# A graph-attention layer on one core: TensorE turns the edge features after k and q, three turns ahead

## The chip, the core and the metric

The kernel runs on one core of one Trainium2 chip. Its engines work side by side, each on its own list of instructions, in order: TensorE (PE: matrix products and transposes through the array, results in PSUM), VectorE (DVE), ScalarE (ACT), GpSimd (POOL) and SyncE (SP). They wait for one another through semaphores. SP issues nearly all plain transfers here, GpSimd the gathers. The metric is device time in microseconds: before the change 2678.94 us, the median of three runs (2676.61 to 2681.4).

## The reference

A graph has 12,500 nodes and 212,500 edges, sorted by destination. Nodes are normalized, and q and v are products of them; k is a product of the edges' features. Per edge and head (8 heads of 16) there are three logits: q of the source with k, q of the destination with k, and q of the source with q of the destination. Each goes through a softmax over the edges of one destination, and their sum weighs v.

```python
h = jnp.maximum(_layernorm(x, axis=-1), 0.0)
q = (node_h @ Wq.T + bq).reshape(N, NUM_HEADS, HEAD_DIM)
k = (edge_h @ Wk.T + bk).reshape(-1, NUM_HEADS, HEAD_DIM)
v = (node_h @ Wv.T + bv).reshape(N, NUM_HEADS, HEAD_DIM)
qs, qd = (q[src], q[dst])
in_m = jnp.sum(qs * k, axis=-1)
out_m = jnp.sum(qd * k, axis=-1)
diag_m = jnp.sum(qs * qd, axis=-1)
score = (_segment_softmax(in_m * SCALE, dst, N) + _segment_softmax(out_m * SCALE, dst, N) + _segment_softmax(diag_m * SCALE, dst, N)) * att
h = jax.ops.segment_sum(score[..., None] * v[dst], dst, num_segments=N)
out = h @ Wo.T + bo          # x + leaky_relu(out) is the result
```

## The kernel before

The kernel prepares q for all nodes and writes it to a table in HBM, then walks the edges in 415 turns of 512 edges (128 partitions by 4). Turn g belongs to stage t = g // 5 and stretch s = g % 5: the edges are cut into five long stretches, and a stage takes one block of each.

The instructions of an engine stand in the order in which the program makes them: `pin` chains each to the one before on its engine, so nothing is reordered by a scheduler. What a turn does for its 512 edges:

- `turn` (L1308, L1310): TensorE transposes four tiles of edge features `ea` into the one PSUM buffer `eT_ps`; ScalarE copies them to `eT` (three buffers).
- `project` (L1317, L1318): TensorE multiplies `eT` with wk, which gives k in one half of `qk_ps` (two buffers), and adds the bias.
- `spread_q` (L1326, L1329): TensorE multiplies one-hots `oh` of the destinations with a window of 42 nodes' q, which gives the destinations' q in the other half of `qk_ps`; ScalarE copies that half to `qd`.
- `logits` (L1337, L1339, L1340): VectorE multiplies the gathered source q `qq`, `qd` and k by pairs and sums over each head. This frees `qk_ps` for the turn after next.
- `one_hots` (L702, L703): two instructions on ScalarE, three turns ahead.

The order of the loop before is: transposes of turn g+2, k of g+1, the destinations' q of g+1, logits of g, one-hots of g+3. So TensorE's list has the transposes ahead of k, and ScalarE's list has the copy of features, then the copy to `qd`, then the one-hots.

Behind these five come odd jobs, which depend on s. They belong to earlier stages. At s = 0 TensorE transposes the first logits of a block (`turn_head`, L1368) and VectorE scans; at s = 1 VectorE scans backwards; at s = 2 TensorE transposes the maxima (`turn_max`, L1443), VectorE subtracts (L1452) and ScalarE takes exponentials (L1453); at s = 3 TensorE makes `d_ps` (L1485), from which ScalarE makes the selection `sel` (L1488, L1489); at s = 4 TensorE sums the edges of a node into `w_ps` (`to_rows`, L1499), ScalarE copies these to `rows` (L1504), which SP stores (L1520), and TensorE transposes logits (`turn_logits`, L1360). Work on nodes (`nodes_before`, `nodes_between`, for instance L1228, L1239, L1242, L1247) and on parts of the q table (L1619) is spread over the turns as well.

The gathers run 26 turns ahead: `gather(g + LOOK)` issues four indirect transfers from GpSimd (L711), each of 128 rows of q. They are tied to TensorE by hand. The dictionary `behind` keeps two of TensorE's instructions for each turn: entry 0 is its last product after `project`, entry 2 its last product after the odd jobs. In turn g the first of the four gathers waits for entry 0 of g, the third for entry 2 of g, and both entries of g were made in turn g-1:

```python
held = behind.get((g - LOOK, j), held)
...
behind[g + 1, 0] = pinned[products]
...
behind[g + 1, 2] = pinned[products]
```

SP's list holds, by turns, the load of edge features six turns ahead (`fetch_edges`, L691, six buffers `ea`), of windows (L685), and the stores of `rows`.

Of the kernel before, what the change touches and what calls it, by code (L numbers as in the profile page):

```python
# [472 lines left out]
def ordered_path(ctx: ExitStack, tc: tile.TileContext, flag, x, src, dst, edge_attr, edge_weight,  # L473
# [88 lines left out]
    def pin(inst):  # L562

        engine = str(inst.ins.engine)
        if engine in pinned:
            tc.add_manual_dep(inst.ins, pinned[engine], mybir.DependencyInfo(
                mybir.DependencyClass.NoSync, mybir.DependencyReason.DATA), reason="in order")
        pinned[engine] = inst.ins.name
        return inst
# [61 lines left out]
    end = S * G  # L631
# [5 lines left out]
    def load_sources(t):  # L637
        if t < G:
            sources[t] = load.tile([P, S, JN], I32, name="sources", bufs=IDX)
            pin(nc.sync.dma_start(  # L640
                sources[t], src[:end * BE].rearrange("(s b p j) -> p s b j", s=S, b=G, p=P)[:, :, t, :]))
# [80 lines left out]
    def raw_rectify(g):  # L722
        for j in range(JN):
            row = qqs[g][:, j, :]
            pin(nc.scalar.activation(row, row, AF.Relu, bias=raw["shift"][:, g, j:j + 1],
                                     scale=raw["inv"][:, g, j:j + 1]))
# [53 lines left out]
    with tc.tile_pool(name="prep", bufs=1) as prep, \  # L780
# [359 lines left out]
        for g in range(-2, GN):  # L1140
# [13 lines left out]
            for of in range(RAW):  # L1154
                turn = (5 * of - 30) // 4
# [35 lines left out]
    class Nodes:  # L1191
# [45 lines left out]
        def turn(self, to):  # L1237
            for b in range(self.n):
                pin(nc.tensor.transpose(to[:, b, :], self.h[:, b, :], ident))  # L1239
            if self.hT is None:  # L1240
                self.hT = fin.tile([P, JN, P], F32, name="hT")
            pin(nc.scalar.copy(self.hT[:, :self.n], to[:, :self.n]))  # L1242
# [57 lines left out]
    with tc.tile_pool(name="work", bufs=2) as work, \  # L1300
# [21 lines left out]
        def spread_q(g):  # L1322
            s, d = g % S, st[g // S]
            qd_ps = qks[g][:, 1]
            for j in range(JN):
                pin(nc.tensor.matmul(qd_ps[:, j, :], ohs[g][:, j * P:(j + 1) * P],  # L1326
                                     d["win"][:, s, :], start=(j == 0), stop=(j == JN - 1)))
            qds[g] = work.tile([P, JN, F], F32, name="qd")
            pin(nc.scalar.copy(qds[g], qd_ps))  # L1329
            del ohs[g]  # L1330

        def logits(g):
            s, t = g % S, g // S
            if s == 0:
                lTs[t] = scan.tile([P, JN, S, H3], F32, name="lT", bufs=4)
            prod = work.tile([P, JN, 3, F], F32, name="prod", bufs=1)
            pin(nc.vector.tensor_mul(prod[:, :, 0:2, :].rearrange("p j i f -> p i j f"),  # L1337
                                     qqs[g][:, None].to_broadcast([P, 2, JN, F]), qks[g]))
            pin(nc.vector.tensor_mul(prod[:, :, 2, :], qds[g], qks[g][:, 0]))  # L1339
            pin(nc.vector.tensor_reduce(lTs[t][:, :, s, :],  # L1340
                                        prod.rearrange("p j i (h d) -> p j (i h) d", d=DIM), AX.X,
                                        ALU.add))
            del qks[g], qds[g], qqs[g]
# [398 lines left out]
        project(0)  # L1742
        spread_q(0)
        turn(1)
        raw_rectify(SOON)
        for g in range(end):
            s, t = g % S, g // S
# [3 lines left out]
            fetch_edges(g + EDGES)  # L1751
            if s == 1:
                load_sources(t + IDX)
            if g + 2 < end:
                turn(g + 2)
            if g + 1 < end:
                project(g + 1)
                behind[g + 1, 0] = pinned[products]
                spread_q(g + 1)
            logits(g)  # L1760
            one_hots(g + 3)
            if s == 0:
# [157 lines left out]
```

## Time and profile before

| | |
|---|---|
| median of the runs | 2678.94 us |
| profiled execution | 2685.56 us, span 2683.8 us |
| PE, PEld | 1794.6 us (67%), 1479.8 us (55%) |
| DVE | 2046.8 us (76%) |
| ACT | 1397.2 us (52%) |
| POOL | 1587.5 us (59%) |
| granted TensorE clock, mean | 0.739 |
| HBM | 132 GB/s over the span |

PE stands for TensorE's products and transposes, PEld for its weight loads, which overlap them. "Idle before, releaser" in a row is the time in which the engine did nothing ahead of these instructions, and what ended most of it; "issue" means that the profile shows nothing to wait for, and "remote" that the releaser is not known. Ends of TensorE's products are modelled; those of the others are recorded. A view by windows gives the busy time of each engine in a stretch, with the number of its instructions.

### The profile page before, as it was taken

The numbers are of one execution on the slowest core, as the hardware profiler recorded it, in microseconds if no ns is written. First come the engines' busy times: TensorE is split into PE (matmuls) and PEld (weight loads), VectorE is DVE, ScalarE is ACT, GpSimd is POOL, SyncE is SP. The second block draws the span as 40 slices with busy tenths as digits, with TensorE's granted clock in tenths as the row PEclk, the third lists the DMA queues.
The fourth block names the chain that finished last, engine by engine and source line by source line (L and its number), as shares of the span: only waits on it lengthen the run. The fifth ranks groups of instructions, "written<-read, shape, count | busy, mean of one in ns | idle before, by whom it ended". The sixth has DMA issues, their size and how long they took to land.

```text
span 2683.8 us, 36827 instructions
## 1 busy us (share of the span) xinstructions
PE 1794.6 (67%) x10958; PEld 1479.8 (55%) x10958; DVE 2046.8 (76%) x2496; ACT 1397.2 (52%) x2663; POOL 1587.5 (59%) x1683
## 2 busy tenths in 40 slices
PE   3656766666566666676666766676767676766775
PEld 2455655555455545565555655565656565555664
DVE  4648887777787878787778877777877787778995
ACT  3647754454455554554545545455545554455672
POOL 6656566666666666666666666666666666666100
PEclk6767877777777777777777777766777677677786
DMA  6656444444555454454444444454444444444321
GB/s 184 175 159 169 124 129 136 136 128 133 141 146 135 127 151 135 135 139 136 127 130 129 133 130 129 131 136 130 115 135 134 125 129 131 133 129 129 112 87 53
DMA packets 379084, 355.75 MB, mean 133 GB/s; under 512 B 192913, under 2 KB 298779, under 8 KB 378669
## 3 DMA queue, kind: packets, MB, share of 16 engines
q1 hardware_dynamic: 309963, 238.05, 31.2%
q0 software_dynamic: 53184, 108.92, 15.5%
q10 hardware_dynamic: 15728, 6.33, 1.0%
q8 instruction: 90, 1.47, 0.2%
q14 instruction: 119, 0.97, 0.1%
HBM read 320.89 MB, written 32.17 MB: 132 GB/s over the span
## 4 chain that ended last, share of the span: by engine, by line
PE 39%; ACT 17%; DVE 16%; issue 12%; another core or an unknown queue 12%; DMA 1%; POOL 1%; DVEq 1%; SPq 0%; ACTq 0%; POOLq 0%
PE qk_ps L1317 11%; PE eT_ps L1308 8%; PE w_ps L1499 6%; DVE lT L1340 4%; DVE prod L1337 4%; PE qk_ps L1326 4%; ACT qd L1329 3%; ACT relb L702 3%; ACT oh L703 2%; ACT eT L1310 2%; DVE prod L1339 2%; PE node_ps L1247 2%; PE m_ps L1443 2%; PE l_ps L1360 1%
## 5 line engine op out<-in xcount | busy, mean ns | idle before, releaser
L711 POOL DMA_INDIRECT qq<-q_table,sources x1564 | 1482.0, 948 | 856.3 <-issue 375.1
L1337 DVE TENSOR_TENSOR prod<-qq,qk_ps 128x1024 f32<-128x1024 f32 x412 | 501.2, 1217 | 318.6 <-ACT qd L1329 185.1
L1340 DVE TENSOR_REDUCE lT<-prod 128x96 f32<-128x1536 f32 x415 | 727.5, 1753 | 14.3
L1317 PE MATMUL qk_ps<-wk,eT 128*128 128x128 f32 x3320 | 597.0, 337 | 72.2 <-issue 34.3
L1329 ACT COPY qd<-qk_ps 128x512 f32<-128x512 f32 x415 | 244.2, 589 | 731.2 <-remote 241.8
L1317 PEld LDWEIGHTS qk_ps<-wk,eT 128*128 128x128 f32 x3320 | 551.9, 250 | 90.8 <-issue 43.0
L1308 PE MATMUL eT_ps<-ident,ea 128*128 128x128 f32 x1660 | 347.1, 345 | 373.6 <-ACT eT L1310 169.0
L1308 PEld LDWEIGHTS eT_ps<-ident,ea 128*128 128x128 f32 x1660 | 241.9, 176 | 469.3 <-ACT eT L1310 193.5
L1310 ACT COPY eT<-eT_ps 128x512 f32<-128x512 f32 x415 | 240.0, 578 | 200.4 <-remote 114.3
L1499 PE MATMUL w_ps<-back,sel 128*126 128x144 f32 (+1 forms) x1296 | 229.3, 350 | 159.1 <-issue 141.7
L1499 PEld LDWEIGHTS w_ps<-back,sel 128*126 128x126 f32 (+1 forms) x1296 | 211.8, 240 | 173.5 <-issue 157.5
L702 ACT ACTIVATE relb<-relb,before 126x512 bf16<-126x512 bf16 x415 | 301.9, 728 | 0.0
L1339 DVE TENSOR_TENSOR prod<-qd,qk_ps 128x512 f32<-128x512 f32 x415 | 282.1, 680 | 0.0
L703 ACT ACTIVATE oh<-relb 126x512 bf16<-126x512 bf16 x415 | 261.3, 630 | 13.2
L1326 PE MATMUL qk_ps<-win,oh 126*128 126x128 bf16 x1660 | 194.8, 250 | 6.8 <-issue 6.8
L1326 PEld LDWEIGHTS <-oh 126*128 126x128 bf16 x1660 | 110.5, 109 | 32.4 <-issue 8.0
L1443 PE MATMUL m_ps<-ident,m 120*128 120x120 f32 x332 | 74.6, 360 | 68.9 <-issue 46.9
L1400 DVE TENSOR_TENSOR_SCAN l_ps<-far,carry,l_ps 120x512 f32<-120x512 bf16 x80 | 102.5, 1281 | 11.1 <-PE eT_ps L1308 7.5
L711 POOL DMA_INDIRECT qq<-in_x_dram,sources x84 | 80.0, 952 | 49.3 <-issue 22.3
L1452 DVE TENSOR_TENSOR back<-lT,m_ps 128x480 f32<-128x480 f32 x83 | 53.9, 650 | 70.9 <-remote 38.0
L1431 DVE TENSOR_TENSOR_SCAN m<-far,head,l_ps 120x512 f32<-120x512 bf16 x81 | 102.9, 1271 | 0.0
L1443 PEld LDWEIGHTS m_ps<-ident,m 120*128 120x128 f32 x332 | 52.3, 215 | 81.9 <-issue 57.7
(252 smaller groups left out, 1783.0 us busy)
## 6 DMA issues: line engine op xcount, KB each, us to landing
ea<-in_edge_attr_dram SPq DMA_DIRECT2D x415, 256.0 KB
relb<-rel_d SPq DMA_DIRECT2D x83, 630.0 KB
qq<-q_table,sources POOLq DMA_INDIRECT x1564
win<-q_table SPq DMA_DIRECT2D x415, 31.5 KB
far<-far_d SPq DMA_DIRECT2D x84, 120.2 KB
q_table<-q SPq DMA_DIRECT2D x24, 384.0 KB
sums<-rows SPq DMA_DIRECT2D x411, 7.9 KB
q_table<-xq SPq DMA_DIRECT2D x24, 256.0 KB
```

The lines of the kernel that those rows point to most:

```text
L702: pin(nc.scalar.activation(d, d, AF.Abs, bias=before[:K3]))
L703: pin(nc.scalar.activation(oh, d, AF.Relu, bias=1.0, scale=-1.0))
L711: rows = pin(nc.gpsimd.indirect_dma_start(out=qq[:, j, :], out_offset=None, in_=x if g < RAW else q_table, in_offset=bass.IndirectOffsetOn ...
L1308: pin(nc.tensor.transpose(eT_ps[:, j, :], eas[g][:, j * F:(j + 1) * F], ident))
L1310: pin(nc.scalar.copy(eT, eT_ps))
L1317: pin(nc.tensor.matmul(k_ps[:, j, :], eTs[g][:, j, :], wk, start=(j == 0), stop=False))
L1326: pin(nc.tensor.matmul(qd_ps[:, j, :], ohs[g][:, j * P:(j + 1) * P], d["win"][:, s, :], start=(j == 0), stop=(j == JN - 1)))
L1329: pin(nc.scalar.copy(qds[g], qd_ps))
L1337: pin(nc.vector.tensor_mul(prod[:, :, 0:2, :].rearrange("p j i f -> p i j f"), qqs[g][:, None].to_broadcast([P, 2, JN, F]), qks[g]))
L1339: pin(nc.vector.tensor_mul(prod[:, :, 2, :], qds[g], qks[g][:, 0]))
L1340: pin(nc.vector.tensor_reduce(lTs[t][:, :, s, :], prod.rearrange("p j i (h d) -> p j (i h) d", d=DIM), AX.X, ALU.add))
L1499: pin(nc.tensor.matmul(w_ps[:(hi - lo) * W, lo:hi].rearrange("p s c -> p (s c)"), d["sel"][:n, j, lo:hi, :].rearrange("p s w -> p (s w)"), ...
```

## The change

`project` and `spread_q` of turn g+1 come first in a turn, and then `turn`, now of g+3 in place of g+2. One more set of features is turned ahead of the loop. The rest of the loop is the same; the copy of features now stands behind the copy to `qd` in ScalarE's list, and ahead of the one-hots. Entry 0 of `behind` is the same instruction as before. Entry 2 is too, except in turns in which no odd job of TensorE comes behind: there it is the last transpose in place of the last product of `spread_q`.

```diff
         spread_q(0)
         turn(1)
+        turn(2)
         raw_rectify(SOON)
         for g in range(end):
...
             if s == 1:
                 load_sources(t + IDX)
-            if g + 2 < end:
-                turn(g + 2)
             if g + 1 < end:
                 project(g + 1)
                 behind[g + 1, 0] = pinned[products]
                 spread_q(g + 1)
+            if g + 3 < end:
+                turn(g + 3)
             logits(g)
             one_hots(g + 3)
```

## The prediction

> **What bounds the kernel now.** I read the page first, then two windows (the loop with gathers, the loop without), then the loop's groups, then single stretches of the timeline.
>
> ```profile
> span 2683.8 us, 36827 instructions
> ```
>
> Two rows of the view by windows (busy us and instructions of PE, PEld, DVE, ACT, POOL, then granted clock, DMA share, GB/s):
>
> ```profile
> 300.00:2400.00 2100.00, 1415.48 (x8663) 1172.72 (x8661) 1635.36 (x1742) 1076.75 (x2001) 1340.40 (x1415) 0.74 0.48 133
> 2500.00:2600.00 100.00, 78.69 (x548) 66.35 (x548) 95.83 (x104) 70.33 (x138) 1.67 (x4) 0.83 0.35 103
> ```
>
> No engine is full in the first row, and in the second, where GpSimd has no gathers left, TensorE issues 548 products per 100 us instead of 8663/21 = 412. The gathers, 26 turns ahead of their use, pace the loop: four belong to a turn, and 2100/1415 x 4 = 5.94 us is the turn. The groups of 300 to 2400 us:
>
> ```profile
> L711 POOL DMA_INDIRECT qq<-q_table,sources x1415 | 1340.5, 947 | 762.9 <-issue 339.8 <-remote 142.8 <-PE eT_ps L1308 60.3
> L1308 PE MATMUL eT_ps<-ident,ea 128*128 128x128 f32 x1420 | 299.0, 347 | 357.4 <-ACT eT L1310 164.5 <-issue 118.7 <-ACT hT L1242 39.4
> L1329 ACT COPY qd<-qk_ps 128x512 f32<-128x512 f32 x355 | 209.0, 589 | 656.4 <-remote 203.9 <-PE m_ps L1443 129.7 <-PE qk_ps L1326 112.7
> L1504 ACT COPY rows<-w_ps 126x144 f32<-126x144 f32 x71 | 19.4, 273 | 99.3 <-PE eT_ps L1308 41.7 <-PE l_ps L1360 25.8 <-PE qk_ps L1318 11.9
> ```
>
> A gather takes 0.947 us. Its idle is of two kinds, a steady 0.30 us and long pauses; rows of GpSimd's timeline show both (last column: idle before, and what ended it):
>
> ```profile
> 1045.02 0.95 POOL L711 DMA_INDIRECT qq<-q_table,sources  x1 [2.22 <-remote]
> ...
> 1051.28 0.94 POOL L711 DMA_INDIRECT qq<-q_table,sources  x1 [0.30 <-issue]
> 1053.96 0.95 POOL L711 DMA_INDIRECT qq<-q_table,sources  x1 [1.74 <-PE qk_ps L1326]
> ...
> 1060.21 0.95 POOL L711 DMA_INDIRECT qq<-q_table,sources  x1 [0.30 <-issue]
> 1062.74 0.95 POOL L711 DMA_INDIRECT qq<-q_table,sources  x1 [1.59 <-PE m_ps L1443]
> ```
>
> ```profile
> 1387.23 0.94 POOL L711 DMA_INDIRECT qq<-q_table,sources  x1 [1.88 <-remote]
> ...
> 1395.98 0.94 POOL L711 DMA_INDIRECT qq<-q_table,sources  x1 [0.30 <-issue]
> 1398.98 0.94 POOL L711 DMA_INDIRECT qq<-q_table,sources  x1 [2.05 <-remote]
> ```
>
> ```profile
> 1171.05 0.94 POOL L711 DMA_INDIRECT qq<-q_table,sources  x1 [1.67 <-PE w_ps L1499]
> ...
> 1174.79 0.94 POOL L711 DMA_INDIRECT qq<-q_table,sources  x1 [0.30 <-issue]
> 1177.30 0.95 POOL L711 DMA_INDIRECT qq<-q_table,sources  x1 [1.57 <-PE node_ps L1239]
> ```
>
> Gathers come in runs and stop for a product of TensorE. A run of six with its pause takes 1053.96 - 1045.02 = 8.94 us, the next 8.78; a run of eight 11.75; a run of four 6.25. Per gather that is 1.48, 1.47, 1.56. The longer the run the longer the pause, so six or eight hardly differ; four costs 6% more.
>
> Why does GpSimd stop for products that TensorE issued long ago? Around the pause at 1397 us, on TensorE, ScalarE and VectorE:
>
> ```profile
> 1391.62 0.61 PE L1326 MATMUL qk_ps<-win,oh 126*128 126x128 bf16 x4
> 1392.43 1.08 PE L1443 MATMUL m_ps<-ident,m 120*128 120x120 f32 x4 [0.20 <-DVE m L1431]
> ...
> 1394.15 1.19 PE L1317 MATMUL qk_ps<-wk,eT 128*128 128x128 f32 x8
> ```
>
> ```profile
> 1398.01 0.59 ACT L1329 COPY qd<-qk_ps 128x512 f32<-128x512 f32 x1 [7.81 <-remote]
> ```
>
> ```profile
> 1398.74 0.66 DVE L1452 TENSOR_TENSOR back<-lT,m_ps 128x480 f32<-128x480 f32 x1 [2.87 <-remote]
> ```
>
> The q products are over at 1392.23 by the record, yet their copy starts at 1398.01, 1.09 us after the last gather ended (1395.98 + 0.94); VectorE (m_ps, over at 1393.51) and GpSimd go on at 1398.74 and 1398.98. Three engines that wait for TensorE are let go together once the gathers pause. Without gathers the copy follows at once, 0.04 us after the products' end:
>
> ```profile
> 2526.47 0.40 PE L1326 MATMUL qk_ps<-win,oh 126*128 126x128 bf16 x4
> ...
> 2526.91 0.59 ACT L1329 COPY qd<-qk_ps 128x512 f32<-128x512 f32 x1 [0.72 <-PE qk_ps L1326]
> ```
>
> So I read: while gathers run back to back, word of TensorE's results reaches the others late; a pause lets it through. What TensorE issued before a pause is then known, and that sets the next run.
>
> The Trainium skill, "SBUF — State Buffer", section Who interferes with whom, says that "PE and ACT never wait on anyone". The rows differ: issue does go on, but results are heard 5.8 us late beside gathers. By the rule the wait at 1398.01 would have another cause; rival D prices that.
>
> **The change part by part.** Follow TensorE's stream. Before, turn g is: transposes of g+2, k of g+1, q of g+1, the turn's odd jobs (scans' transposes, d_ps, w_ps, node work). The next turn begins with the transposes of g+3. After, it is: k of g+1, q of g+1, transposes of g+3, odd jobs. Read as one stream, the only thing that moves is that the transposes of g+3 with their copy go ahead of turn g's odd jobs (and on ScalarE also ahead of the one-hots of g+3). k still follows the odd jobs and the same earlier transposes.
>
> 1. *Counts.* 415 turns, the same instructions: 0. Three sets of transposes stand before the loop instead of two: one set and copy, 1.12 + 0.59 us by rows below, are earlier there and gone later. Between 0 (hidden by the gathers running) and +1.7; I take 0.
>
> 2. *ScalarE.* The copy of the features no longer waits behind one-hots, sel, rows:
>
> ```profile
> 1049.65 0.60 ACT L1329 COPY qd<-qk_ps 128x512 f32<-128x512 f32 x1
> 1050.12 0.74 ACT L702 ACTIVATE relb<-relb,before 126x512 bf16<-126x512 bf16 x1
> 1050.90 0.63 ACT L703 ACTIVATE oh<-relb 126x512 bf16<-126x512 bf16 x1
> 1053.67 0.41 ACT L1504 COPY rows<-w_ps 126x144 f32<-126x144 f32 x2 [2.14 <-PE qk_ps L1318]
> 1053.97 0.59 ACT L1310 COPY eT<-eT_ps 128x512 f32<-128x512 f32 x1
> ```
>
> ```profile
> 1045.33 1.12 PE L1308 MATMUL eT_ps<-ident,ea 128*128 128x128 f32 x4 [3.38 <-ACT eT L1310]
> ...
> 1051.34 0.60 PE L1308 MATMUL eT_ps<-ident,ea 128*128 128x128 f32 x4
> ...
> 1054.62 0.66 PE L1308 MATMUL eT_ps<-ident,ea 128*128 128x128 f32 x4
> ```
>
> The transposes recorded at 1051.34 are copied only at 1053.97, because `rows` of the same turn waits for the pause, and the next transposes (one buffer) wait for that copy. After the change that copy stands ahead of `rows` and of 0.74 + 0.63 us of one-hots: about 1.4 us earlier in every turn, 4 us in one turn of five. The other way, the copy now stands behind `qd`, whose wait is the longest on ScalarE (656.4 us). For a stalled `qd` of turn h the old order has copied eT of h+1, and so has the new: same lead. What TensorE gets is at most the 164.5 us that its transposes idle for that copy (357.4 for anything). Off the pace of the gathers this is worth nothing by itself; it counts only where products get issued before a pause that were not before.
>
> 3. *The gathers' waits.* Of the four gathers of turn g the first waits for k's last product of turn g, the third for TensorE's last product by that point of turn g-1. The first wait keeps its place. The third now has transposes in front of its odd job, and in the one turn of five without an odd job (s = 1) it waits for the transposes instead of the q products. They need the copy of the set before, so for a `qd` that is stuck they are not issued by the pause, while the old order had the odd job issued. Cost between 0 (they get through in the run: issued about 0.59 + 0.59 us of copies and 1.12 us of transposes = 2.3 us after the pause ends, in a run that starts with a third gather the next third one comes 4 x 1.25 = 5.0 us later) and a run of eight or six cut to four. I take: mostly through, since 2.3 is under 5.0.
>
> 4. *Odd jobs.* d_ps, m_ps, h_ps, w_ps come up to one stall of the transposes later: 0 to 3.38 us, the idle of the row at 1045.33. Behind them stand `sel` and `rows` on ScalarE, `back` and the scans on VectorE, SP's store of rows. The pause hides this where it ends after them. I take 0.
>
> 5. *Edge features.* They are transposed one turn (5.9 us) sooner after their load, and their buffer comes free one turn sooner:
>
> ```profile
> L1308 PE MATMUL eT_ps<-ident,ea x1660: 269/328/477, 158.1 to 2608.5; 128*128 128x128 f32 x185
> L691 SPq DMA_DIRECT2D ea<-in_edge_attr_dram x415: 2/366/1839, 118.6 to 2581.2; - x139
> ```
>
> The lead at the ends is 39.5 and 27.3 us, so over 21 us stay. 256 KB at the 133 GB/s of the window take 2 us: 0. SP's other issues keep their order.
>
> *Sum.* Rounds of five turns, 20 gathers, run now for example as 6 + 8 + 6: 8.86 x 2 + 11.75 = 29.5 us (8.86 is the mean of the two runs of six shown, between which `rows` waits for the pause). If part 2 lets all runs be eight, a gather costs 1.469 us instead of 2100/1415 = 1.484: 1564 x 0.015 = 24 us saved (1564 gathers from q_table, 1415 of them in the window). I take 0.4 of it, about 10 us, since part 3 works against it: against the profiled execution's own 2685.56 us (its span and 1.8 around it) 2675.6, and as that one stands 6.6 above the median 2678.94, 2669 for the median.
>
> **The rivals.**
>
> B, hidden. Six and eight cost nearly the same (1.48, 1.47), so pauses may merely move. For it: the pause grows with the run. Against it: runs of four exist. 2674 to 2684, middle 2679. (0.2%, 5 us, is about what a measurement of this kernel can tell from no change.)
>
> C, slower: the third gather's wait. Word of the transposes does not get through in the run, so one run of eight per round becomes two of four. Round: 2 x 8.86 + 2 x 6.25 = 30.2 instead of 29.5, 0.75 us in each of 1564/20 = 78 rounds: +58, 2737. In one round of five: +12, 2691. It decides once more than one round in ten has such a cut (+6). For it: word already issued is known to stay out for 5.8 us (row at 1398.01), and 2.3 us after a pause is not at once. Against: in the old order word of the transposes does get through inside a run:
>
> ```profile
> 1049.18 0.58 ACT L1310 COPY eT<-eT_ps 128x512 f32<-128x512 f32 x1
> ```
>
> This copies the transposes recorded at 1045.33 to 1046.45, in the middle of the run that began at 1045.02, and 4.2 us into it, under the 5.0 that part 3 allows.
>
> D, much faster: results are never late, and the waits come from ScalarE's order alone. Then the 164.5 us of transposes waiting for the copy lie on the path: 2678.94 - 164.5 = 2514. Against: the copy at 1398.01 waits with its own products long issued. This is what the skill's sentence above would lead to.
>
> **How the numbers follow.** A (a little faster, 2645 to 2673) 0.43; B 0.17; C 0.38; D 0.02. The time is A's, 2669. Faster is A and D, 0.45; same 0.17; slower 0.38. A's lower end is the 24 us of all-eight runs and 10 more, for gathers outside the window that stop more often. The range 2645 to 2735 leaves out D and what lies at the far ends of C and A, some 0.15 together.
>
> **What would show it.** Part 2: L1308's idle ended by the copy falls well below 164.5 us, and eT copies stand ahead of `rows`. Part 3: pauses ended by eT_ps before a third gather. A: the gathers' idle in 300 to 2400 us falls by about 10 us per 1415; C: it rises by 10 to 55 with more runs of four. Part 4 is wrong if VectorE's idle before `back` or the scans grows. I am wrong altogether if turns lengthen while the gathers' idle does not, or if the stretch after 2500 us, where VectorE is 96% busy, gets longer.

## The result and the profile after

The changed kernel takes 2724.52 us (median of four runs, 2716.37 to 2729.96), the kernel before 2677.78 us: a ratio of 1.0178, 95% interval 1.016 to 1.0196. It is slower by 1.8%, inside the region of rival C (2691 to 2737). Repeated in another session the ratio was 1.0187 (1.016 to 1.0215).

The profiled execution took 2716.37 us, 30.8 more than the profiled one before. Its page begins, and the same two windows read (columns as before):

```profile
span 2714.6 us, 36828 instructions
```

```profile
300.00:2400.00 2100.00, 1376.57 (x8499) 1141.66 (x8497) 1606.97 (x1711) 1052.66 (x1955) 1312.05 (x1389) 0.74 0.47 130
2500.00:2600.00 100.00, 73.49 (x508) 61.05 (x507) 95.76 (x103) 63.91 (x119) 19.51 (x22) 0.82 0.44 124
```

Gathers still pace the loop: 1389 in 2100 us in place of 1415, so 6.05 us per turn in place of 5.94, 1.9% more. The granted clock is 0.74 in both. The groups of 300 to 2400 us after:

```profile
L711 POOL DMA_INDIRECT qq<-q_table,sources x1389 | 1312.9, 945 | 788.9 <-issue 325.7 <-remote 182.6 <-PE l_ps L1360 115.3
...
L1308 PE MATMUL eT_ps<-ident,ea 128*128 128x128 f32 x1388 | 280.2, 337 | 418.1 <-issue 205.7 <-ACT eT L1310 203.7 <-ACT qd L1329 8.5
...
L1329 ACT COPY qd<-qk_ps 128x512 f32<-128x512 f32 x348 | 202.3, 581 | 744.4 <-remote 382.4 <-PE qk_ps L1326 189.0 <-PE qk_ps L1318 93.2
...
L1499 PE MATMUL w_ps<-back,sel 128*126 128x144 f32 x559 | 147.1, 438 | 126.6 <-issue 56.3 <-ACT sel L1489 42.9 <-ACT sel L1488 27.3
...
L1452 DVE TENSOR_TENSOR back<-lT,m_ps 128x480 f32<-128x480 f32 x69 | 44.9, 651 | 106.4 <-PE m_ps L1443 23.7 <-PE d_ps L1485 19.1 <-PE eT_ps L1308 17.4
...
L1504 ACT COPY rows<-w_ps 126x144 f32<-126x144 f32 x70 | 19.1, 273 | 73.1 <-PE l_ps L1360 49.0 <-PE w_ps L1499 21.5 <-issue 1.4
```

GpSimd idles 26 us more ahead of 26 fewer gathers. The named releaser that grew most is `l_ps`, TensorE's transposes of logits at s = 4: 115.3 us. Before, the view of that line's waiters had

```profile
  POOL qq L711: 10.2, 8
```

and among the groups of before, these two answer to `w_ps` and `back` above (the others stand in the prediction):

```profile
L1499 PE MATMUL w_ps<-back,sel 128*126 128x144 f32 x568 | 132.4, 399 | 135.9 <-issue 124.3 <-ACT sel L1489 5.8 <-DVE prod L1337 4.5
...
L1452 DVE TENSOR_TENSOR back<-lT,m_ps 128x480 f32<-128x480 f32 x70 | 45.5, 650 | 64.8 <-remote 32.5 <-PE d_ps L1485 15.6 <-PE eT_ps L1308 5.1
```

So `w_ps` now waits 70 us for `sel` (5.8 before), though its whole idle is not longer (126.6 us, 135.9 before), and VectorE's idle ahead of `back` grew by 42 us.

To see where the pauses stand, each pause of GpSimd (idle over 0.35 us between two gathers) was put to the turn whose gather it stopped, from the records of L711, over the same 340 turns in each kernel. "First" and "third" are the gathers of a turn that wait for TensorE. The third of a turn with s = 2 waits for what TensorE issued last at s = 1, and so on.

| pauses: number, us | before | after |
|---|---|---|
| time of 340 turns | 2018.1 us | 2055.5 us |
| all | 215, 380.8 | 232, 426.6 |
| ahead of first gathers | 141, 261.6 | 96, 175.5 |
| ahead of third gathers | 69, 116.5 | 131, 248.2 |
| of these at s = 2 | 3, 5.9 | 35, 61.4 |
| of these at s = 4 | 0, 0.0 | 22, 44.2 |
| of these at s = 0 | 47, 78.2 | 63, 130.1 |
| over 2.5 us | 3, 8.8 | 21, 63.0 |
| pauses that began with the product made | 173, 314.4 | 161, 284.1 |
| time in pauses, product not yet made | 27.9 us | 104.7 us |
| of it ahead of third gathers at s = 0 | 17.8 us | 92.8 us |

For the last three rows the recorded end of the product that a first or third gather waits for was set against the end of the gather before it. Up to that product's end it is a late product that holds GpSimd; what the pause lasts beyond it is late word to GpSimd. (A product can be late because word to another engine was: the example at s = 0 below.)

Two thirds of what the third gathers add (132 us) is given back at the first gathers (86 us): a pause at a third gather makes one at the next first gather needless. What is left is 46 us, and it lies in 18 more pauses over 2.5 us (54 us more): of those under 2.5 us there are 212 before (372.0 us) and 211 after (363.6 us). The last rows say what these long pauses are. Time spent on late word fell, by 31 us; time in which TensorE had not yet made the product rose by 77 us, 75 of them at the third gathers of s = 0, which wait for `l_ps`. The 340 turns are 37.4 us longer and the whole execution 30.8.

**A third gather at s = 2.** Rows of TensorE, ScalarE and GpSimd from the timeline after:

```profile
1574.98 0.40 PE L1326 MATMUL qk_ps<-win,oh 126*128 126x128 bf16 x4
...
1575.21 0.60 PE L1308 MATMUL eT_ps<-ident,ea 128*128 128x128 f32 x4
...
1581.36 0.58 ACT L1329 COPY qd<-qk_ps 128x512 f32<-128x512 f32 x1 [5.94 <-issue]
1581.56 0.94 POOL L711 DMA_INDIRECT qq<-q_table,sources  x1 [0.30 <-issue]
...
1584.23 0.58 ACT L1310 COPY eT<-eT_ps 128x512 f32<-128x512 f32 x1 [2.28 <-remote]
...
1584.46 0.94 POOL L711 DMA_INDIRECT qq<-q_table,sources  x1 [1.96 <-remote]
```

The turn is one with s = 1. Its q products (1574.98) are heard of at 1581.36, within a run of eight gathers. Its transposes, over at 1575.81, are heard of only in the pause that begins at 1582.50: ScalarE goes on at 1584.23, GpSimd at 1584.46, 8.65 us after their end. In the kernel before, the third gather of such a turn waits for the q products, and word of these was in here before the run ended.

**A third gather at s = 0**, some twelve microseconds on:

```profile
1596.12 0.59 ACT L1310 COPY eT<-eT_ps 128x512 f32<-128x512 f32 x1 [2.95 <-remote]
...
1597.89 0.91 ACT L1488 ACTIVATE sel<-d_ps 128x420 f32<-128x420 f32 x2
1598.84 0.90 ACT L1489 ACTIVATE sel<-sel 128x840 f32<-128x840 f32 x1
...
1599.79 3.57 PE L1499 MATMUL w_ps<-back,sel 128*126 128x144 f32 x16 [1.92 <-ACT sel L1489]
...
1603.15 1.06 PE L1360 MATMUL l_ps<-ident,lT 128*120 128x128 f32 x4
...
1604.48 0.94 POOL L711 DMA_INDIRECT qq<-q_table,sources  x1 [3.38 <-PE l_ps L1360]
```

The copy of the features waits for a pause; `sel` stands behind it and behind the one-hots; `w_ps` waits for `sel`, `l_ps` comes behind `w_ps`, and the third gather waits for `l_ps`. This pause is not one of late word: TensorE has not issued `l_ps` yet when the run of four ends.

The two examples belong together. On the stop at s = 2 follow a run of eight, a stop at the third gather of s = 4 (1596.42), and a run of only four. Of the 63 stops at third gathers of s = 0, 21 come four gathers after a stop at s = 4, and these have 53.7 of the 92.8 us; 13 of the 21 follow, like this one, a stop at the third gather of s = 2. Before, no stop came about in this way.

### The profile page after: what moved, and what is told of

It is laid out like the page before. It is cut to its first block, busy times and chain, and to the rows that moved or that the text cites. A ratio compares the mean times of both kernels' runs of the same rounds, so it can differ in the third digit from the quotient of the medians.

```text
span 2714.6 us, 36828 instructions
## 1 busy us (share of the span) xinstructions
PE 1774.9 (65%) x10958; PEld 1463.1 (54%) x10958; DVE 2048.6 (75%) x2496; ACT 1398.1 (52%) x2663; POOL 1586.4 (58%) x1683
## 4 chain that ended last, share of the span: by engine, by line
PE 34%; DVE 19%; ACT 15%; another core or an unknown queue 15%; issue 13%; DMA 1%; DVEq 1%; POOL 1%; SPq 0%; ACTq 0%; POOLq 0%
PE qk_ps L1317 10%; PE w_ps L1499 7%; DVE prod L1337 5%; DVE lT L1340 4%; PE eT_ps L1308 4%; PE qk_ps L1326 4%; ACT qd L1329 3%; ACT eT L1310 3%; ACT relb L702 3%; DVE prod L1339 2%; ACT oh L703 2%; PE m_ps L1443 2%; PE l_ps L1360 1%; PE qk_ps L1318 1%
## 5 line engine op out<-in xcount | busy, mean ns | idle before, releaser
L711 POOL DMA_INDIRECT qq<-q_table,sources x1564 | 1478.7, 945 | 900.0 <-issue 366.6
L1340 DVE TENSOR_REDUCE lT<-prod 128x96 f32<-128x1536 f32 x415 | 727.4, 1753 | 14.3
L1337 DVE TENSOR_TENSOR prod<-qq,qk_ps 128x1024 f32<-128x1024 f32 x412 | 501.1, 1216 | 294.1 <-ACT qd L1329 143.9
L1317 PE MATMUL qk_ps<-wk,eT 128*128 128x128 f32 x3320 | 580.3, 329 | 157.5 <-issue 74.6
L1317 PEld LDWEIGHTS qk_ps<-wk,eT 128*128 128x128 f32 x3320 | 521.5, 238 | 212.7 <-issue 103.2
L1308 PE MATMUL eT_ps<-ident,ea 128*128 128x128 f32 x1660 | 331.6, 335 | 449.7 <-ACT eT L1310 220.4
L1308 PEld LDWEIGHTS eT_ps<-ident,ea 128*128 128x128 f32 x1660 | 224.3, 172 | 481.2 <-ACT eT L1310 237.1
L1499 PE MATMUL w_ps<-back,sel 128*126 128x144 f32 (+1 forms) x1296 | 259.5, 385 | 140.3 <-issue 59.7
L1499 PEld LDWEIGHTS w_ps<-back,sel 128*126 128x126 f32 (+1 forms) x1296 | 241.5, 270 | 165.7 <-issue 70.4
L1326 PE MATMUL qk_ps<-win,oh 126*128 126x128 bf16 x1660 | 186.9, 241 | 10.1 <-issue 10.1
L1326 PEld LDWEIGHTS <-oh 126*128 126x128 bf16 x1660 | 105.8, 105 | 36.2 <-issue 12.4
L711 POOL DMA_INDIRECT qq<-in_x_dram,sources x84 | 82.2, 979 | 41.4 <-issue 23.2
L1318 PE MATMUL qk_ps<-b,ones 3*128 3x32 bf16 x415 | 90.4, 218 | 2.8 <-issue 2.8
```

Of the source, the lines that this page charges most:

```text
L711: rows = pin(nc.gpsimd.indirect_dma_start(out=qq[:, j, :], out_offset=None, in_=x if g < RAW else q_table, in_offset=bass.IndirectOffsetOn ...
L1308: pin(nc.tensor.transpose(eT_ps[:, j, :], eas[g][:, j * F:(j + 1) * F], ident))
L1317: pin(nc.tensor.matmul(k_ps[:, j, :], eTs[g][:, j, :], wk, start=(j == 0), stop=False))
L1340: pin(nc.vector.tensor_reduce(lTs[t][:, :, s, :], prod.rearrange("p j i (h d) -> p j (i h) d", d=DIM), AX.X, ALU.add))
L1499: pin(nc.tensor.matmul(w_ps[:(hi - lo) * W, lo:hi].rearrange("p s c -> p (s c)"), d["sel"][:n, j, lo:hi, :].rearrange("p s w -> p (s w)"), ...
```

## The experiments

All ratios are against the kernel before on the same chip in the same session. The five sessions ran on five chips, of which one differs: there the kernel before takes 2168.39 us, on the other four 2676.56 to 2679.56. Points of loss are counted from the changed kernel's first ratio, 1.0178.

| | median | ratio | 95% interval |
|---|---|---|---|
| e1: s = 1 waits for q | 2692.1 | 1.0051 | 1.0037 to 1.0066 |
| e2: transposes behind odd jobs | 2676.31 | 0.9989 | 0.9978 to 1.0 |
| e3: copy as before | 2748.69 | 1.0258 | 1.0234 to 1.0282 |
| e4: d_ps first at s = 3 | 2705.02 | 1.0101 | 1.007 to 1.0131 |
| e8: e1 and e4 | 2691.36 | 1.0076 | 1.0047 to 1.0105 |
| e9: third gathers wait for q | 2716.68 | 1.0136 | 1.009 to 1.0182 |
| e10: the same in the kernel before | 2674.68 | 1.0002 | 0.9988 to 1.0015 |
| e11: the change again | 2726.69 | 1.0187 | 1.016 to 1.0215 |
| e12: e9 and e4 | 2693.78 | 1.0054 | 1.0034 to 1.0074 |
| e13: e8, and jobs first at s = 4 | 2686.43 | 1.0023 | 1.0008 to 1.0037 |
| e14: e2, one-hots last | 2672.18 | 0.997 | 0.9959 to 0.9982 |
| e15: e2, third gathers wait for q | 2681.47 | 1.001 | 0.9994 to 1.0027 |
| e16: before, plain transfers | 2186.31 | 0.8165 | 0.8151 to 0.8179 |
| e17: after, plain transfers | 2185.02 | 0.8162 | 0.8148 to 0.8176 |
| on the chip of 2168.39 us: | | | |
| e5: as e8 | 2168.15 | 0.9999 | 0.999 to 1.0009 |
| e6: as e13 | 2166.64 | 0.9993 | 0.9984 to 1.0003 |
| e7: as e9 | 2169.68 | 1.0006 | 0.9996 to 1.0016 |
| b7: as e10 | 2168.07 | 1.0001 | 0.9992 to 1.0011 |

In what was expected, T1 says that the loss comes from odd jobs that stand late behind the transposes (Part 4), T2 that it comes from the third gather's wait for the transposes at s = 1 (Part 3, rival C), T3 that ScalarE's new list costs it (the copy of the features behind `qd`, Part 2).

**e1, the wait at s = 1 alone undone.**

```diff
                 spread_q(g + 1)
+                q_last = pinned[products]
             if g + 3 < end:
                 turn(g + 3)
+            t_last = pinned[products]
...
-            behind[g + 1, 2] = pinned[products]
+            behind[g + 1, 2] = q_last if pinned[products] == t_last else pinned[products]
```

> The changed kernel, but in turns without an odd job of TensorE the third gather waits for the q products again, not for the transposes. Theory 1 (odd jobs stand behind the transposes, so d_ps, sel, w_ps and l_ps come late, and the third gather of the turn s = 0, which waits for l_ps, stops longer): it stays slow, 2710 to 2730. Theory 2 (the third gather's new wait for transposes in the turn s = 1): back to 2675 to 2690.

It gives back 1.27 of the 1.78 points. The pauses at the third gathers of s = 2 fall from 35 to 6, and 22 runs of ten gathers appear, which neither kernel had; those over 2.5 us fall from 21 to 14, and the time of products not yet made from 104.7 to 56.9 us. At 2692.1 it stays 2 us above what T2 expects. So far T2 is right for the larger part; the rest, 0.5%, is not this wait.

**e2, the transposes of g+3 behind the odd jobs.**

```diff
-            if g + 3 < end:
-                turn(g + 3)
             logits(g)
...
             behind[g + 1, 2] = pinned[products]
+            if g + 3 < end:
+                turn(g + 3)
```

> The changed kernel, but the transposes of g+3 stand behind turn g's odd jobs on TensorE, and their copy behind those of ScalarE. Theories 1 and 2: back to the time before, 2670 to 2690, with the pause ahead of the third gather of s = 0 as before. If three ahead in place of two costs by itself (buffers, loads of edge features): 2700 or more.

The loss is gone (0.9989), and the time of products not yet made is 24.4 us. Read as one stream, this is nearly TensorE's old order; the third set turned ahead of the loop, and the transposes ahead of the node work between turns, are still in it and cost nothing. The place of the transposes, and of their copy, ahead of the odd jobs does; e3 tells the two apart.

**e3, TensorE's list as after, ScalarE's as before.** `turn` keeps its transposes; the copy is issued at the head of the next turn.

```diff
-            eT = work.tile([P, JN, P], F32, name="eT", bufs=3)
-            pin(nc.scalar.copy(eT, eT_ps))
-            eTs[g] = eT
+            turned_ps[g] = eT_ps
...
+        def keep(g):
+            if g in turned_ps:
+                eT = work.tile([P, JN, P], F32, name="eT", bufs=3)
+                pin(nc.scalar.copy(eT, turned_ps.pop(g)))
+                eTs[g] = eT
...
+            keep(g + 2)
             if g + 1 < end:
                 project(g + 1)
```

> TensorE's list as in the changed kernel, ScalarE's list as before (the copy of the features waits for the head of the next turn, behind one-hots and odd jobs). Theory 1 (TensorE's order is the cause): slow, 2705 to 2740. Theory 3 (ScalarE's order is the cause: the copy behind the copy to qd, ahead of one-hots and sel, makes sel late): back to 2670 to 2690.

It is slower still, by 0.8 points, and above what T1 expects too. TensorE's transposes wait more for their buffer (its group from 300 to 2400 us; the lines of this kernel are 6 higher):

```profile
L1308 PE MATMUL eT_ps<-ident,ea 128*128 128x128 f32 x1380 | 292.9, 349 | 657.3 <-ACT eT L1316 359.8 <-issue 214.0 <-ACT q L1617 30.8
```

359.8 us in place of 203.7, and products not yet made hold the gathers for 128.8 us. T3 falls: with TensorE's new order, ScalarE's new list is the good half of the change.

**e4, at s = 3 alone `d_ps` and `sel` ahead of the transposes.**

```diff
-            if g + 3 < end:
+            if g + 3 < end and s != 3:
                 turn(g + 3)
...
                 later(show_ends, t - 2)
+                if g + 3 < end:
+                    turn(g + 3)
```

> The changed kernel, but in the turns s = 3 alone d_ps, and sel on ScalarE, go ahead of the transposes and their copy. Theory 1: most of the loss is back, 2675 to 2700, and w_ps waits little for sel. Theories 2 and 3: 2710 to 2730.

It gives back 0.77 points, less than T1 allows and more than T2 and T3 do. Pauses over 2.5 us fall from 21 to 4 (63.0 to 14.0 us), but the number of pauses does not (232). So it is late `d_ps` and `sel` that make the pauses long. `l_ps`, still behind the transposes of s = 4, is late as before: 89.9 us at the third gathers of s = 0, in place of 92.8. The edit also does something that T1 leaves out. Entry 2 of s = 3 is now the last transpose, as these come behind `d_ps`, so the third gather of s = 4 waits for transposes (22 stops, as in the changed kernel). This is a wait of the kind that e1 takes out; e5, e6, e8 and e13 have it too (e6 and e13 also for the third gather of s = 0).

**e5, e6, e7, b7: the same questions on the other chip.** e5 is e1 and e4 together, e6 has the odd jobs first at s = 4 too, e7 lets the third gather of every turn wait for the q products, b7 does so in the kernel before:

```diff
                 spread_q(g + 1)
+                q_last = pinned[products]
...
-            behind[g + 1, 2] = pinned[products]
+            behind[g + 1, 2] = q_last
```

> Both mendings of the changed kernel at once: at s = 1 the third gather waits for the q products, at s = 3 d_ps and sel go ahead of the transposes. If the two causes are separate (late third gather 1.3 points of 1.8, late sel 0.8 points), they add up to a little under the time before: 2665 to 2685. If the pauses only move about, it stays where the first mending alone is, 2688 to 2700.

> As the run with both mendings, and at s = 4 w_ps and the transposes of logits go ahead of the transposes of features too, so that these are ahead of odd jobs at s = 0 and 2 alone. If l_ps behind the transposes is what holds the third gather of s = 0: 2655 to 2678. If not: as with both mendings.

> The changed kernel, but in every turn the third gather waits for the q products of the turn before and no longer for odd jobs or transposes. If the whole loss comes through the third gather's wait: 2660 to 2690. If late odd jobs cost through ScalarE and VectorE as well: 2695 to 2720. If freer gathers keep TensorE's word out longer, so that the first gather stops longer: over 2700 with pauses ahead of first gathers.

> The kernel before with the same freer third gather. If odd jobs hold the gathers there too: faster, 2640 to 2670. If runs of gathers merely get longer and pauses with them: same, 2670 to 2690. If the wait is needed so that TensorE's word gets out: slower, 2690 or more.

None of them differs from the kernel before there. Window, groups and timeline of e5:

```profile
300.00:1900.00 1600.00, 1218.24 (x8330) 1003.00 (x8329) 1561.33 (x1676) 1035.54 (x1924) 1210.73 (x1278) 0.83 0.62 164
```

```profile
L711 POOL DMA_INDIRECT qq<-q_table,sources x1278 | 1212.2, 949 | 389.6 <-issue 260.6 <-DMA qq<-q_table,sources 30.5 <-PE qk_ps L1326 15.5
...
L1329 ACT COPY qd<-qk_ps 128x512 f32<-128x512 f32 x342 | 199.0, 582 | 378.2 <-PE qk_ps L1326 365.8 <-PE qk_ps L1318 6.4 <-DVE lT L1340 3.4
```

```profile
1010.24 0.94 POOL L711 DMA_INDIRECT qq<-q_table,sources  x1 [0.30 <-issue]
...
1010.84 0.40 PE L1326 MATMUL qk_ps<-win,oh 126*128 126x128 bf16 x4
...
1011.27 0.58 ACT L1329 COPY qd<-qk_ps 128x512 f32<-128x512 f32 x1 [2.28 <-PE qk_ps L1326]
1011.48 0.95 POOL L711 DMA_INDIRECT qq<-q_table,sources  x1 [0.30 <-DVE lT L1340]
```

A gather takes 0.949 us (0.947 in the kernel before on its chip) with the same 0.30 us between two, but there is not one pause. Four gathers take 4 x 1.25 = 5.0 us; the loop itself goes faster, 343 turns in the 1600 us (L1337 counted), 4.66 us each, and uses up the gathers' lead. VectorE is busy 1561 of 1600 us. The copy to `qd` starts 0.03 us after the products' end, with gathers running; so do, within 0.04 us, all 174 copies to `qd` of the window for which ScalarE was idle (in the kernel before, on its chip, 300 to 1900 us, the median of 155 is 2.19 us). The late word on which the prediction and the change turn does not exist on this chip. The change itself did not run there.

**e8 to e11, on a chip where word is late.** The same kernels as e5, e7 and b7, and the change again.

> The changed kernel with both parts of the loss mended: entry 2 (the third gather's wait) stays on the q products in the turns s = 1, and at s = 3 d_ps and sel stand ahead of the transposes and their copy. On a chip where the kernel before takes some 2678 us: if the loss is the sum of the two waits (1.27 and 0.77 points apart), 2665 to 2685, ratio 0.995 to 1.003, and the pauses ahead of the third gathers of s = 2 and s = 0 are as few as before. If pauses only move to the next gather that waits for TensorE, 2688 to 2715, ratio 1.004 to 1.014. On a chip where it takes 2168 us: ratio 0.998 to 1.002 by either, as the first look at this kernel gave 0.9999 there.

> The changed kernel with the third gather of every turn waiting for the q products alone, never for transposes or odd jobs. On a chip where the kernel before takes some 2678 us: if the third gathers' waits are the whole loss, it is as fast as the kernel before with the same freer wait (within 0.5%), and 2660 to 2690. If the order also costs through the late copy, sel and rows themselves, it stays 0.5% or more behind that kernel, 2690 to 2715. On a chip where it takes 2168 us: ratio 0.998 to 1.002.

> The kernel before with the third gather of every turn waiting for the q products alone. On a chip where the kernel before takes some 2678 us: if each cut of a run at a third gather costs what the pauses say (46 pauses of 1.66 us ahead of the third gather of s = 0 alone), some 10 to 40 us faster, 2640 to 2668; if pauses only move, 2672 to 2684. On a chip where it takes 2168 us: ratio 0.998 to 1.002.

> The changed kernel itself, in the same session as the other three. On a chip where the kernel before takes some 2678 us: ratio 1.015 to 1.020, as measured, which is the base for the other three. On a chip where it takes 2168 us, where TensorE's word is prompt beside the gathers: if the loss comes from that late word, ratio 0.998 to 1.002; if it comes from the order of TensorE's work as such, 1.01 to 1.02 there too.

The two cures do not add up: 1.0076, within the intervals no better than e1 alone; but the second brings the wait at s = 4 with it, which stops 23 third gathers here (18 in e1, there for `d_ps`). The long pauses are gone (1 over 2.5 us, from 25 in the change again), but 227 pauses stay, against 215 in the kernel before.

e9 was the surprise. No third gather waits for transposes or odd jobs any more, and 1.36 points of loss remain; in the kernel before the same freedom is worth nothing (1.0002), since the pauses move to the first gathers. Taking the wait away is then not the cure that e1 seemed to show. e9's pauses are as few as before (214), but 12 of them last over 2.5 us, 55.5 us together, all ahead of first gathers. One of 8.94 us, from the timelines of TensorE, ScalarE and GpSimd:

```profile
1217.00 0.53 PE L1485 MATMUL d_ps<-shows,ends_t 21*128 21x420 bf16 x2
...
1222.97 0.59 ACT L1310 COPY eT<-eT_ps 128x512 f32<-128x512 f32 x1 [4.35 <-remote]
...
1224.74 0.91 ACT L1488 ACTIVATE sel<-d_ps 128x420 f32<-128x420 f32 x2
...
1225.30 0.58 PE L1245 MATMUL node_ps<-b,ones 3*128 3x512 bf16 x1 [7.77 <-ACT sel L1488]
...
1229.52 0.23 PE L1318 MATMUL qk_ps<-b,ones 3*128 3x32 bf16 x1
...
1230.03 0.95 POOL L711 DMA_INDIRECT qq<-q_table,sources  x1 [8.94 <-PE qk_ps L1318]
```

A node product waits 7.77 us for `sel` to have read `d_ps`; `sel` stands behind the copy of the features and the one-hots, and the copy waited for the pause. k stands behind the node product, and the first gather waits for k.

**e12, e13: is that chain the rest?** e12 is e9 with e4's edit; e13 is e8 with the transposes behind the odd jobs at s = 4 too, which are `w_ps` and `l_ps` (the expectation names `m_ps` for the second):

```diff
                     later(turn_logits, t - 1)
+                if g + 3 < end:
+                    turn(g + 3)
```

> The changed kernel with the third gather of every turn waiting for the q products alone, and at s = 3 d_ps and sel ahead of the transposes and their copy. The question is what still cost 1.36 points when the third gathers were free: its trace has pauses of 4.6 to 8.9 us ahead of the first gather of s = 0, where a node product waits for sel, sel waits behind the copy of the features on ScalarE, and k stands behind the node product on TensorE. On a chip where the kernel before takes some 2678 us: if that chain is it, those pauses go (some 22 us of them) and the time is 2685 to 2702, ratio 1.003 to 1.009; if the free third gathers themselves cost the time, 2705 to 2725, ratio 1.010 to 1.018. On a chip where it takes 2168 us: 0.998 to 1.002 by either.

> The changed kernel with entry 2 on the q products at s = 1, and the transposes behind the odd jobs at s = 3 (behind d_ps and sel) and s = 4 (behind w_ps and m_ps). On a chip where the kernel before takes some 2678 us: the kernel without the s = 4 part stood at 1.0076; if what is left is odd jobs late behind the transposes, w_ps and m_ps in time bring it to 2670 to 2688, ratio 0.998 to 1.004; if what is left comes from the transposes' place at s = 0 to 2, or pauses only move, 2690 to 2702, ratio 1.005 to 1.010. On a chip where it takes 2168 us: 0.998 to 1.002 by either.

For the most part, yes. e12 gives back 0.8 points of e9's 1.36, and its pauses over 2.5 us are 4 in place of 12. e13 comes to 1.0023, from e8's 1.0076: with the wait at s = 1 undone and the transposes behind the odd jobs at s = 3 and 4, nearly all of the loss is gone, though third gathers of s = 4 still stop 26 times.

**e14, e15: is there a better version?** Both have the transposes behind the odd jobs (e2). e14 moves `one_hots(g + 3)` behind them, so ScalarE does its odd jobs and copies the features ahead of the one-hots; e15 lets third gathers wait for the q products.

```diff
-            one_hots(g + 3)
...
             if g + 3 < end:
                 turn(g + 3)
+            one_hots(g + 3)
```

> The changed kernel with the transposes of three ahead behind all odd jobs on TensorE, and the one-hots behind the copy of the features on ScalarE: the old order of TensorE's stream with the part of ScalarE's new order that goes with it. On a chip where the kernel before takes some 2678 us: if the earlier copy is worth on its own what it was worth in the changed kernel (0.8 points), 2650 to 2668, ratio 0.990 to 0.997; if it was worth something only because TensorE's order made the transposes late, 2670 to 2684, ratio 0.997 to 1.003. On a chip where it takes 2168 us: 0.998 to 1.002.

> The changed kernel with the transposes of three ahead behind all odd jobs on TensorE, and the third gather of every turn waiting for the q products alone. On a chip where the kernel before takes some 2678 us: the two parts alone stood at 0.9989 and 1.0002; if the freer wait takes pauses away once TensorE is not late, 2645 to 2668, ratio 0.988 to 0.997; if a longer run only brings a longer pause, 2668 to 2682, ratio 0.997 to 1.002. On a chip where it takes 2168 us: 0.998 to 1.002.

e14 is faster than the kernel before by 0.3%, the best of all, on the border between the two expectations. Its 340 turns have 231 pauses, as many as the changed kernel's, but 380.3 us of them and one over 2.5 us: the number of pauses is not the price, their length is, and products not yet made have only 14.3 us. Whether the copy or the odd jobs gain by going ahead of the one-hots is not told apart. Its groups:

```profile
L711 POOL DMA_INDIRECT qq<-q_table,sources x1421 | 1344.3, 946 | 758.1 <-issue 327.2 <-remote 126.1 <-PE qk_ps L1326 89.7
...
L1308 PE MATMUL eT_ps<-ident,ea 128*128 128x128 f32 x1420 | 299.7, 345 | 368.0 <-issue 216.1 <-ACT eT L1310 135.1 <-ACT back L1453 15.4
```

e15 shows no gain. Its pauses are those of e2 in number and sum (222, 380.0 us, against 222, 383.4); they have only moved from third gathers (63 to 22) to first ones (154 to 195).

**e16, e17: without gathers from the table.** GpSimd issues plain transfers of 128 neighbouring rows of q at the same places, with the same waits; each edge gets some other node's q.

```diff
-                rows = pin(nc.gpsimd.indirect_dma_start(
-                    out=qq[:, j, :], out_offset=None, in_=x if g < RAW else q_table,
-                    in_offset=bass.IndirectOffsetOnAxis(
-                        ap=sources[g // S][:, g % S, j:j + 1], axis=0)))
+                if g < RAW:
...
+                else:
+                    at = (g * JN + j) * P % (NP - P)
+                    rows = pin(nc.gpsimd.dma_start(qq[:, j, :], q_table[at:at + P, :]))
```

> The kernel before with plain transfers of 128 neighbouring rows of q, issued by GpSimd at the same places with the same waits, in place of the indirect gathers from the table (so the output is not the reference's: each edge gets some other node's q). On a chip where the kernel before takes some 2678 us: if the late word of TensorE comes from the indirect gathers, the pauses go and the time comes to 2150 to 2300 us, near the 2168 us of the prompt chip; if it comes from any transfers that GpSimd issues, or from the chip itself whatever GpSimd does, the pauses stay and the time is 2550 to 2700 us.

> The changed kernel with the same plain transfers in place of the gathers (output not the reference's, as there). Against the kernel before with plain transfers: if the change's loss is a matter of late word, and that goes with the gathers, the two are within 0.3%; if late word stays, the changed one is 1.0 to 2.0% slower than the other; if the order costs by itself, without late word, also 1.0 to 2.0% slower, and then with no long pauses of GpSimd in its trace.

On one of the four chips that agree (the kernel before takes 2676.84 us there) both come to 2186 and 2185 us, near the 2168 us of the other chip, and they are alike: with prompt word, and VectorE as the bound, the changed order costs nothing. What it would cost with prompt word if GpSimd set the pace is not shown. Window, groups and timeline of e16, whose lines are 4 to 7 higher:

```profile
300.00:1900.00 1600.00, 1228.54 (x8356) 1014.28 (x8356) 1566.83 (x1689) 1029.85 (x1928) 729.56 (x1374) 0.82 0.61 169
```

```profile
L718 POOL DMA_DIRECT2D qq<-q_table x1374 | 729.7, 537 | 872.9 <-PE qk_ps L1322 586.1 <-PE l_ps L1364 172.4 <-PE m_ps L1447 70.4
...
L1333 ACT COPY qd<-qk_ps 128x512 f32<-128x512 f32 x344 | 202.1, 588 | 343.1 <-PE qk_ps L1330 338.3 <-DVE lT L1344 2.9 <-DVE prod L1341 0.8
```

```profile
1004.56 0.40 PE L1330 MATMUL qk_ps<-win,oh 126*128 126x128 bf16 x4
...
1004.92 2.12 POOL L718 DMA_DIRECT2D qq<-q_table  x4 [0.41 <-PE qk_ps L1322]
1004.99 0.59 ACT L1333 COPY qd<-qk_ps 128x512 f32<-128x512 f32 x1 [0.78 <-PE qk_ps L1330]
```

GpSimd's transfers move the same bytes in the same number of packets, each issue takes 0.537 us in place of 0.947, and the copy to `qd` follows the products' end by 0.03 us while transfers are issued. GpSimd still stops, for 872.9 us, but for products just made: all 284 first transfers of the window that stopped began 0.30 or 0.31 us after the end of their k. In the kernel before, the 115 first gathers that stopped from 300 to 1900 us began a median of 5.8 us after it. VectorE is the bound (1566.83 of 1600 us; 343 turns, as in e5).

**The runs side by side.** The time in which gathers were held by a product not yet made, over the same 340 turns, is 14.3 us in e14, 24.4 in e2, 27.9 in the kernel before, 36.2 in e13, 56.9 in e1, 43.4 in e8, 99.0 in e4, 104.7 in the changed kernel and 128.8 in e3. The runs stand here in the order of their ratios; only e1 and e8, whose intervals overlap, would change places. The four in which all third gathers wait for the q products are in the order of their ratios too: 13.0 us in e10, 19.6 in e15, 50.4 in e12, 61.7 in e9.

## Why the prediction was wrong

**What bounds the kernel** held: the pace of the gathers fell by 1.9%, and the time rose by 1.8%. That late word of TensorE makes most pauses held too, and more sharply than was argued: e16 takes the gathers away, and with them the late word and 490 us.

**Part 1 and Part 5**, both taken as 0, held. For Part 1, e2 has three sets turned ahead and stands at 0.9989. Part 5 had its size wrong: the features are not transposed one turn (5.9 us) sooner. Only the odd jobs of one turn lie between the old place and the new, and from the issue of the load to the transposes it is 19.5 us in place of 22.0 (means of 320 turns), 2.5 us sooner. The profile names no load among what the transposes waited for.

**Part 2** had the sign of ScalarE's list right: e3 says that it is worth 0.8 points in the new order, and e14 that one-hots behind the copy and the odd jobs are worth 0.3% (0.18 to 0.41) in the old, 8 us, where 10 were forecast. That the sizes are near is no proof, as e14 also puts the odd jobs ahead of the one-hots. The sign in the profile was no sign: the transposes' idle for the copy rose from 164.5 to 203.7 us, but it is 210.1 in e2, which loses nothing, and 106.5 in e9, which loses 1.36%.

**Part 3 is one step that failed.** "Mostly through, since 2.3 is under 5.0" counted when the transposes are issued, and took one copy, 4.2 us into a run, for the rule by which their word arrives. The transposes at 1575.21 were issued in time and heard of 8.65 us late. At s = 2 the third gather was stopped in 35 of 68 rounds, so rival C's price, 0.75 us a round, gives 0.75 x 78 x 35/68 = 30 us; e1 gives back 1.27%, 34 us. The sizes agree, but by luck. Rival C has a run of eight cut to two of four, and in both kernels there are 75 runs of eight in the 340 turns (sixes fell from 104 to 92, fours rose from 17 to 29). Nor did late word cost more: the pauses that began with the product made fell from 314.4 to 284.1 us. As far as the runs show, the stops at s = 2 cost through what they move: the next stops fall so that `l_ps` is not made in time, and e1 nearly halves that time (104.7 to 56.9 us). The 22 stops at third gathers of s = 4 were named (the odd job behind the transposes) but not priced; e13 still has 26 of them and loses 0.23%.

**Part 4 is the other, and here the time was spent.** "The pause hides this, I take 0" looked at the odd job's own consumers. The odd jobs stand in a list: `sel` behind the copy, `w_ps` and the node product behind `sel`, `l_ps` and k behind them, and the gathers wait for `l_ps` and k. The pause ends after word of these comes, so it does not hide them, it grows: in place of 0, products not yet made hold the gathers 77 us longer in 340 turns, against 31 us less of late word. VectorE's idle ahead of `back` grew from 64.8 to 106.4 us, which the prediction had named as the mark of its error. The mark is not the price: that idle is 148.7 us in e13, which loses 0.23%, and `w_ps` waits 72.1 us for `sel` in e14, the fastest.

What each of the two steps would cost alone is not settled. Undone alone they give 1.27 and 0.77 points of 1.78, undone together 1.1 of 1.87; but the second edit brings a wait of the first kind with it, and the stops at s = 2 act through late `l_ps`, so the two work one behind the other and do not add. Settled is that the cause as a whole is the transposes' place ahead of the odd jobs on TensorE: e2 moves them and their copy back and loses nothing, and e3 moves the copy alone and loses more.

**Rival B**, pauses that merely move, is right about free waits (e10, e15) and about two thirds of what the third gathers added. **Rival D**, results that are never late, fell: 2724 us in place of 2514. But where word is prompt (e16, e17, the chip of e5) every order that ran takes 2167 to 2186 us.

## What to carry to other kernels

Before moving work ahead in an engine's list, write down everything that stands behind the new place on that engine and on the engines that wait for it, down to the instruction that sets the pace: the price was paid by `sel`, `w_ps`, the node product and k, none of which the change touches. Where a wait is on "the last instruction of that engine so far", any reordering changes what is waited for; pin such waits to the instruction that they mean. And when a pause ends several engines' waits at once, look for what withholds the word, here GpSimd's gathers, issued back to back: without them the time falls by 490 us, and no order around them gave more than 8 us.

## What was not expected of the hardware

- *Late word comes with indirect gathers, on four of five chips.* There, a result of TensorE was heard of 8.65 us after its end while GpSimd issued indirect gathers 0.30 us apart. With plain transfers of the same bytes, on one of the four, it was 0.03 us (e16). Since a plain transfer also holds GpSimd only 0.537 us, and leaves it idle for half the time, the runs do not tell whether the indirection or the unbroken run of issues is what delays the word.
- *One chip has no late word at all*, with the same gathers at 0.949 us (0.947 elsewhere): 2168.39 us for the kernel before, 19% less than the 2677.71 of another. Its granted clock is higher (0.83 against 0.74), but so is that of e16 on one of the four (0.82), where word is prompt too; so the higher clock may go with prompt word rather than make it, which no run separates. Why the chip differs stays open.
- The Trainium skill, "SBUF — State Buffer", section Who interferes with whom, says "PE and ACT never wait on anyone", and means the engines' ports to SBUF. ScalarE waited here for word of transposes long over, as until 1584.23. No run shows whether ports have a part in that, so the sentence neither led to rival D, as the prediction has it, nor is contradicted by these rows.
